# One product of every second pair of samples, shared with its neighbour's, split into seven products of halves

## The chip, the cores and the metric

The kernel runs on 1 core of a Trainium2 chip. The metric is the device time of one execution in microseconds (us). Everything is float32 apart from the zeros that clear PSUM banks.

## The reference, cut to what matters

128 samples of shape 128 x 1024 go through two layers. In each layer a sample uses the weights of its role (1 or 2 of 3 in these inputs):

```python
h = gelu(x @ W_down[role] + b_down[role])      # 128x1024 @ 1024x512
y = x + h @ W_up[role] + b_up[role]            # 128x512 @ 512x1024
out = (y - mean(y)) * rsqrt(var(y) + 1e-5) * gamma[role] + beta[role]
```

The result of layer 0 is the input of layer 1.

## The kernel before

Samples are sorted by role on the chip. Each layer has two stages. The **down stage** makes h for octets of samples (and a few left over) and stores it to DRAM transposed ("hq", "hp"). The **up stage**, which the change touches, takes the samples in 65 items `m` (`NSEQ`, `class Up`): 63 pairs of samples of one role and two single samples (m = 35, 36). Only the first 21 pairs are sure to have the top role; from then on the place of the weights (0, 1 or 2 in `up_blocks`) is read from a table into a register.

The up product of a pair is one level of a Winograd scheme. With A(i,k) half k of sample i's h (128 rows, 256 of the inner dimension) and the weight blocks and their sums B11, B21, T2, T1, T3, B22, T4 (256 x 512 each), a pair makes seven products s1 to s7 instead of eight (`products`, from L937). Each is two TensorE matmuls 128x128 by 128x512 (`product`, L878 to L881). s1, s3, s5 and s7 accumulate in one PSUM bank ("b"), s4 and s6 in another ("e"), s2 = A(0,1)*B21 has bank y (`all_banks[6]`) for itself. After every product VectorE adds what the bank holds then to one half (512 columns) of a sample's row block x in SBUF (`begin` L989, `end` L997; `end` also sums the row for the mean). So the next product into a bank has to wait until VectorE has read it. The sum s2 goes to one place only, the left half of the first sample.

Around the products of a pair stand these steps:

- `load` (L908): h from DRAM, by the queue of SP. `load_rest` (L916): the two samples' x, also by SP.
- `winograd_sums` (L873 to L876): four sums of halves of h on GpSimd (POOL); the second one is made in place and is an operand of s4.
- `seeded` (L932): ScalarE (ACT) copies the bias into a bank before the first product of the pair in it; for m < 4 TensorE clears the bank first (`cleared`, L152).
- `squares` (L1088 to L1094): per sample, ACT makes the mean and the sum of squares, and POOL the power -0.5 of the variance.
- `scaled` (L1101): VectorE makes (y - mean) * gamma.
- `stored`: of the first sample ACT multiplies by the power (L1108) and POOL adds beta (L1109); of the second VectorE does both in one instruction (L1111). `away` (L1116 or L306): SP stores the result.

The order of the instructions on each engine is written out: every step is put on a list with a time (`at(time, step)`), the list is sorted, and each engine runs its steps in that order. One unit of that list is 1/7 of a pair's place: `up_base` grows by 7 per pair, while a pair's products stand at +0, +2, ... +12, so the products of two neighbouring pairs alternate on TensorE.

PSUM has eight banks, s to z. "b" goes round over s, t, u and "e" over v, w, x. Each of the four blocks of SBUF that hold a pair's h has 256 columns at its end that nothing uses.

During the first half of layer 0's up stage the kernel also prepares layer 1's down weights (`DownHalf`: eight groups of four sums on POOL, L361 to L364; loads and stores by SP; copies by ACT and sums by VectorE, L379 and L384), during the second half layer 1's up weights (`UpHalf`: ACT and VectorE).

Of the kernel before, what the change touches and what calls it, by code (L numbers as in the profile page):

```python
# [10 lines left out]
F32 = mybir.dt.float32  # L11
# [9 lines left out]
P = 128  # L21
# [6 lines left out]
def kernel(  # L28
# [38 lines left out]
    NSTAGED = 5  # L67
    staged = region("staged", NSTAGED * 1024)

    hd = {}  # L70
# [5 lines left out]
    for s in range(2):  # L76
# [10 lines left out]
    up_scratch = [  # L87
        {t: dram.tile([R, P, 1024], F32, tag=f"u{layer}{t}", name=f"u{layer}{t}") for t in ORDER}
        for layer in range(2)
    ]  # L90
# [387 lines left out]

    def wu(name, place, j):
        at = ORDER.index(name) * 1024 + j * K  # L480
        if isinstance(place, int):
            return up_blocks[:, place, at : at + K]
        return up_blocks[:, ds(place, 1), at : at + K]

# [106 lines left out]

    plain_blocks = {}

    class PlainItem:
# [18 lines left out]
        def prepare(self):  # L613
            self.bias = new_bias(self.layer, None if self.slots[0] < 2 else self.slots[0], self.tag)
            first = turn_of["results"] % 2
            k = (first, 1 - first, 2)[self.nth % 3]
            self.h = results[:, ts(k, 2048)][:, 0 : 4 * self.n].rearrange("p (f c) -> p f c", f=4)
            self.one = len(self.slots) == 1
            if self.one:
                self.bank = all_banks[(2, 0)[self.parity]]  # L620
                self.ps = [self.bank[:, ts(f, P)] for f in range(4)]
            else:
                self.ps = [all_banks[k] for k in ((6, 7, 1, 3), (2, 0, 4, 5))[self.parity]]

# [246 lines left out]
    def winograd_sums(dst, a, engine=nc.gpsimd):  # L871
# [4 lines left out]
        nc.gpsimd.tensor_tensor(dst[:, 2], a12, dst[:, 0], sub)  # L876

    def product(ps, a, w, place, start=False):  # L878
        for j in range(2):
            nc.tensor.matmul(  # L880
                ps, a[:, j], wu(w, place, j), start=start and j == 0, stop=j == 1, skip_group_check=True  # L881
            )

    before_last = []

    class Up:
        def __init__(self, layer, m):
# [8 lines left out]
            self.before_last = layer == 1 and m == NSEQ - 2  # L896

        def load(self):
            n = self.ns * P
# [9 lines left out]

        def load_rest(self):  # L910
            if self.ns == 1:
                self.x = staged[:, 2048 * (self.slot % 2) :][:, 0:1024].rearrange("p (s n) -> p s n", s=1)
            else:
                self.x = up_block("x", self.pair % 3).rearrange("p (s n) -> p s n", s=2)
            for s, src in enumerate(x_of(self.layer, self.slots, ENG.SP)):
                nc.sync.dma_start(self.x[:, s], src)  # L916

# [9 lines left out]
        def seeded(self, t):  # L927
            spare = self.m == 36 and t == "b"
            ps = all_banks[7] if spare else bank(t)
            if self.m < 4 or spare:  # L930
                cleared(ps)
            nc.scalar.copy(ps, self.t["bias"][:, ts("be".index(t), K)])  # L932
            self.ps[t] = ps

        def products(self):
# [39 lines left out]
            def t4():  # L975
                product(ps["e"], A(0, 1), "B22", self.place)
                self.end(0, 1, ps["e"])

            seeds = [(-3.4 if self.m == 0 else -4, lambda: self.seeded("b")), ({35: -1.65, 36: -0.65}.get(self.m, 1.5), lambda: self.seeded("e"))]
            if self.ns == 2:  # L980
                return list(zip(range(0, 14, 2), (s1, s2, s3, s4, s5, s6, s7))) + seeds
# [17 lines left out]
        def finish_last(self):  # L999
# [29 lines left out]
            def begin_bank(item, s, cols, t):  # L1029
                begun[item.m, cols.start] = ps = bank(t)  # L1030
                nc.scalar.copy(ps, item.t["beta"][:, cols])

# [41 lines left out]
        def finish(self):  # L1074
            if self.last:
                return self.finish_last()
            steps = []
            ending = self.layer == 0 and self.m >= NSEQ - 3
            for s in range(self.ns):
                t = (10.4, 12.4)[s] if self.ns == 2 else 6.4  # L1080
# [24 lines left out]
                def stored(s=s, box=box):  # L1105
                    o, v = box["o"], box["v"][:, 0:1]
                    if s == 0 and not self.before_last and not ending:
                        nc.scalar.mul(o, o, v)  # L1108
# [11 lines left out]

                steps += [(t, squares), (t + 1.3, scaled)]
                if ending:
                    steps += [(t + (2.5, 4.65)[s], stored), (t + (3.6, 5.6)[s], away)]
                    continue
                if not (self.before_last and s == 1):
                    steps.append((t + (3.2 if self.before_last else 3.1), stored))
                    steps.append((t + (5.4, 4.2)[s], away))
            return steps
# [15 lines left out]
    for layer in range(2):  # L1144
# [122 lines left out]
        for m in range(NSEQ):  # L1267
            base = up_base[m]
            item = Up(layer, m)
            at(base - 11.5, item.load)  # L1270
            at(base - 7, item.load_rest)

# [6 lines left out]
            if m >= NSEQ - 4:  # L1279
                at(base + 12.9, lambda p=item.pair: up_done("h", p % 4))  # L1280
                if m >= NSEQ - 3:
                    at(base + 17.2, lambda p=item.pair: up_done("x", p % 3))
# [4 lines left out]
            def known(box=box, m=m):  # L1287
                box["r"] = reg(role_at, SEQ[m], [ENG.SP], R - 1)
                box["c"] = reg(two_changed, m, [ENG.SP], 1)

            prev2 = up_base[m - 2]
            at(prev2 + 2.5, known)
            two_pair = SEQ[m - 2] < SLOT_ONE
            for which, time in (
# [7 lines left out]
                )  # L1302

        if layer == 0:
            for part in range(4):
# [80 lines left out]
```

## Time and profile before

| | |
|---|---|
| median of 3 runs | 2996.15 us (2995.8 to 2997.61) |
| the profiled execution: its time | 2997.57 us |
| the profiled execution: its span (first to last instruction) | 2995.2 us |
| TensorE (PE) busy | 2972.2 us |
| VectorE (DVE) busy | 2316.3 us |
| GpSimd (POOL) busy | 2202.6 us |
| ScalarE (ACT) busy | 1285.1 us |
| granted TensorE clock, mean | 0.998 |
| up stage of layer 0 | about 733 to 1510 us |
| up stage of layer 1 | about 2210 to 2986 us |

A float32 matmul shows as two records (MATMUL) with a weight load each (LDWEIGHTS, on "PEld"). The records of successive matmuls overlap, since their ends are modelled, so the cost of a matmul is read from the starts of successive ones, not from the duration of one. In an answer of the timeline the columns are the start, the length, engine, line and operation, the tiles, and how many were merged.

### The profile page before, as it was taken

The page shows a single profiled execution, that of the slowest core. Times are in us where ns is not written, and L with a number is a line of the kernel's source. Part 1 is how long each engine was busy: PE and PEld are TensorE (multiplying, and loading weights), DVE is VectorE, ACT ScalarE, POOL GpSimd, SP SyncE. Part 2 cuts the span into 40 slices and gives each one's busy share as a digit, 9 for nine tenths or more (in the row PEclk, how much of TensorE's full clock was granted, in tenths as well). Part 3 has the DMA queues.
Part 4 walks back from the last instruction along what each step waited for, and adds up shares of the span by engine and source line. Part 5 has one row for each costly group of instructions (what it writes and reads, how often), then busy time and mean ns, then how long its engine had stood idle before and what let it go on. Part 6 is the DMA issues. An engine that isn't in the chain of part 4 may idle for free. (4 is left out here: it accounts for less than half of the span.)

```text
span 2995.2 us, 43088 instructions
## 1 busy us (share of the span) xinstructions
PE 2972.2 (99%) x10284; PEld 1931.4 (64%) x10294; DVE 2316.3 (77%) x4230; ACT 1285.1 (43%) x2832; POOL 2202.6 (74%) x1965
## 2 busy tenths in 40 slices
PE   8999999999999999999999999999999999999999
PEld 6988888887444444444489888888864444444443
DVE  5498988885787787888855888888857777777777
ACT  1144443333555555555522333333335455554554
POOL 2399998886787887777714888888867777767775
PEclk9999999999999999999999999999999999999999
DMA  8789888445878887988797445675476666777664
GB/s 186 199 234 269 269 258 252 149 148 203 293 257 274 268 289 275 314 294 279 258 257 180 144 146 152 183 206 143 132 265 229 221 220 223 276 247 249 221 220 173
DMA packets 379888, 677.96 MB, mean 226 GB/s; under 512 B 39149, under 2 KB 263662, under 8 KB 379642
## 3 DMA queue, kind: packets, MB, share of 16 engines
q1 hardware_dynamic: 372770, 664.67, 70.0%
q0 software_dynamic: 3072, 8.39, 1.2%
q10 hardware_dynamic: 3800, 2.16, 0.3%
q8 instruction: 88, 1.44, 0.2%
q14 instruction: 158, 1.29, 0.1%
HBM read 676.63 MB, written 249.06 MB: 309 GB/s over the span
## 5 line engine op out<-in xcount | busy, mean ns | idle before, releaser
L1094 POOL TENSOR_TENSOR varu<-varu,mhalf 128x1 f32<-128x1 f32 x254 | 320.5, 1262 | 388.1 <-ACT varu L1093 382.2
L1101 DVE SCALAR_TENSOR_TENSOR units<-blocks,meanu,results 128x1024 f32<-128x1024 f32 x249 | 325.8, 1308 | 169.8 <-ACT units L1092 169.5
L579 DVE STREAM_TRANSPOSE blocks<-staged 128x512 f32<-128x512 f32 x400 | 274.7, 697 | 113.2 <-PE bank_x L630 33.4
L1088 ACT ACTIVATE partu<-statu 128x2 f32<-128x2 f32 x254 | 51.6, 203 | 688.8 <-DVE blocks L997 683.9
L880 PE MATMUL bank_u<-wall,blocks 128*128 (+1 forms) x704 | 330.9, 592 | 0.0
L880 PE MATMUL bank_s<-wall,blocks 128*128 (+1 forms) x672 | 316.0, 592 | 0.7 <-ACT bank_s L932 0.4
L763 ACT ACTIVATE results<-results,bcolo 128x256 f32<-128x256 f32 x448 | 227.4, 508 | 206.6 <-DVE results L781 115.3
L1109 POOL TENSOR_TENSOR units<-units,results 128x1024 f32<-128x1024 f32 x125 | 301.8, 2414 | 3.5 <-ACT units L1108 3.5
L880 PE MATMUL bank_t<-wall,blocks 128*128 (+1 forms) x640 | 301.0, 592 | 0.1
L715 POOL TENSOR_TENSOR units<-blocks 128x512 f32<-128x512 f32 x196 | 250.4, 1278 | 68.0 <-DVE blocks L703 44.8
L1111 DVE SCALAR_TENSOR_TENSOR units<-units,varu,results 128x1024 f32<-128x1024 f32 x128 | 294.6, 2302 | 1.3 <-POOL varu L1094 1.3
L1092 ACT ACTIVATE units<-blocks,meanu 128x1024 f32<-128x1024 f32 x250 | 287.1, 1148 | 8.4
L724 POOL TENSOR_TENSOR units<-blocks,units 128x512 f32<-128x512 f32 x196 | 250.4, 1278 | 14.6 <-PE bank_w L730 3.5
L880 PEld LDWEIGHTS bank_u<-wall,blocks 128*128 128x128 f32 x704 | 133.6, 190 | 166.3 <-issue 156.2
L880 PE MATMUL bank_y<-wall,blocks 128*128 (+1 forms) x504 | 236.8, 592 | 0.2
L880 PEld LDWEIGHTS bank_s<-wall,blocks 128*128 128x128 f32 x672 | 127.4, 190 | 161.7 <-issue 150.7
L880 PEld LDWEIGHTS bank_t<-wall,blocks 128*128 128x128 f32 x640 | 121.3, 190 | 153.7 <-issue 143.8
L873 POOL TENSOR_TENSOR blocks<-blocks 128x256 f32<-128x256 f32 x126 | 193.9, 1539 | 24.2 <-DMA blocks<-hq 21.9
L730 PE MATMUL bank_y<-blocks,wall 128*128 128x256 f32 x784 | 201.2, 379 | 0.0
L880 PEld LDWEIGHTS bank_y<-wall,blocks 128*128 128x128 f32 x504 | 95.8, 190 | 119.1 <-issue 118.7
L880 PE MATMUL bank_x<-wall,blocks 128*128 (+1 forms) x352 | 165.4, 592 | 0.0
L730 PEld LDWEIGHTS bank_y<-blocks,wall 128*128 128x128 f32 x784 | 149.0, 190 | 20.3
(310 smaller groups left out, 6570.3 us busy)
## 6 DMA issues: line engine op xcount, KB each, us to landing
staged<-in_x_dram SPq DMA_DIRECT2D x512, 128.0 KB
mid<-units SPq DMA_DIRECT2D x128, 512.0 KB
staged<-mid SPq DMA_DIRECT2D x512, 128.0 KB
blocks<-in_x_dram SPq DMA_DIRECT2D x126, 512.0 KB
blocks<-mid SPq DMA_DIRECT2D x126, 512.0 KB
out_dram<-units SPq DMA_DIRECT2D x125, 512.0 KB
hq<-results SPq DMA_DIRECT2D x112, 512.0 KB
blocks<-hq SPq DMA_DIRECT2D x112, 512.0 KB
```

What stands on the lines that cost most here:

```text
L579: nc.vector.transpose(to[:, :, at_col : at_col + P].rearrange("p j (a t) -> p j a t", t=SQ), v[:, k])
L715: engine.tensor_tensor(d["d1"], m(0, 0), m(1, 0), sub)
L724: engine.tensor_tensor(d["d2"], m(0, 1), d["d0"], sub)
L730: nc.tensor.matmul(ps[:, 0:256], u, v[:, j], start=start and j == 0, stop=stop and j == 1, skip_group_check=True)
L763: nc.scalar.activation(y, y, AF.Gelu, bias=self.bias[:, f : f + 1])
L873: engine.tensor_tensor(dst[:, 1], a11, a21, sub)
L880: nc.tensor.matmul(ps, a[:, j], wu(w, place, j), start=start and j == 0, stop=j == 1, skip_group_check=True)
L1092: nc.scalar.activation(box["o"], self.x[:, s], AF.Square, bias=m, accum_out=v)
L1094: nc.gpsimd.tensor_tensor(v, v, mhalf[:, 0:1], ALU.pow)
L1101: nc.vector.scalar_tensor_tensor(box["o"], self.x[:, s], box["m"][:, 0:1], self.t["gamma"], add, mul)
L1109: nc.gpsimd.tensor_tensor(o, o, self.t["beta"], add)
L1111: nc.vector.scalar_tensor_tensor(o, o, v, self.t["beta"], mul, add)
```

## The change

25 times per layer two neighbouring pairs, the first with odd m (5, 7, ... 27 and 39, 41, ... 63), share their products s2. Both are a left operand 128x256 with the same right operand B21 of 256 x 512; one above the other they are a product 256x256 by 256x512, and that is made as seven products of halves: left operands 128x128, right operands 128x256 (`class Shared`). The four sums of the left operands are made on POOL in a new region `shared_d`; of the right operands, three are quarters of B21 and four are sums t1 to t4, which lie in the free columns of the four h blocks. The sums are made once per place of the weights: for place 0 on the spot, for places 1 and 2 POOL makes them in passing and SP stores them to DRAM; from m = 21 on the first pair of each couple reloads them, each load under the condition that the role changed. The seven products use the next bank of "e", the next of "b" and bank y. ACT copies the first product from one bank to the other. VectorE adds the banks to the left halves of the first samples of both pairs in six additions 128x256.

With that the order of the pairs' other six products changes: the first pair begins with s4 and makes s1 at +6, after the additions of the shared products, since s1 is now the one that finishes the left half (`s1_end`). The first pair's last steps change places: its first sample is finished by VectorE, its second by ACT and POOL (`by_pool`). The second pair's h is loaded earlier, its x loads are apart, and its `scaled` steps stand later. A bank in which only 256 columns were begun is cleared by TensorE before a pair uses it whole again (`whole`). In layer 1 the banks of the first left-over pairs of the down stage, which ran in fixed banks, are chosen so as to avoid those last used.

```diff
+    class Shared:
+        UNITS = ("t1", "t3", "t2", "t4")
+        d = shared_d.rearrange("p (u c) -> p u c", c=P)
...
+        @classmethod
+        def reload(cls, layer, place, cond):
+            for u in range(4):
+                src = shared_scratch[layer][u][ds(place, 1)].rearrange("o p n -> p (o n)")
+                nc.sync.dma_start(cls.tail(u), src, cond=cond, cond_hint=False)
...
+        def m(self, i, k):
+            return (self.first, self.second)[i].a[:, 0, 2 + k]
+        def begin(self):
+            b, e = bank("e"), bank("b")
+            begun_in_part.extend((b, e))
+            self.ps = {"b": b[:, 0:UNIT], "x": all_banks[6][:, 0:UNIT], "e": e[:, 0:UNIT]}
+            if self.first.m in (min(SHARED), LATER):
+                cleared(all_banks[6])
+        def inner(self, name):
+            m, d = self.m, self.d
+            k, i0, i1, op = {
+                "d1": (1, lambda: m(0, 0), lambda: m(1, 0), sub),
+                "d3": (3, lambda: m(1, 0), lambda: m(1, 1), add),
+                "d0": (0, lambda: d[:, 3], lambda: m(0, 0), sub),
+                "d2": (2, lambda: m(0, 1), lambda: d[:, 0], sub),
+            }[name]
+            nc.gpsimd.tensor_tensor(d[:, k], i0(), i1(), op)
+        def product(self, p):
...
+                "p1": ("b", lambda: m(0, 0), lambda: b(0, 0)),
+                "p2": ("x", lambda: m(0, 1), lambda: b(1, 0)),
+                "p3": ("b", lambda: d[:, 0], lambda: t("t2")),
+                "p4": ("e", lambda: d[:, 3], lambda: t("t1")),
+                "p5": ("b", lambda: d[:, 1], lambda: t("t3")),
+                "p6": ("e", lambda: d[:, 2], lambda: b(1, 1)),
+                "p7": ("b", lambda: m(1, 1), lambda: t("t4")),
+            }[p]
+            nc.tensor.matmul(self.ps[to], v(), w(), start=p in ("p1", "p4"), stop=True, skip_group_check=True)
+        def carry(self):
+            nc.scalar.copy(self.ps["x"], self.ps["b"])
+        def flow(self, t, i, h):
+            y = (self.first, self.second)[i].x[:, 0, ts(h, UNIT)]
+            tt(y, self.ps[t], y, add)
+        def steps(self):
+            s = [(-1.9, self.begin), (2.3, self.carry)]
+            s += [(-2.4 + 0.1 * k, lambda n=n: self.inner(n)) for k, n in enumerate(("d3", "d0", "d1", "d2"))]
+            for p, t in dict(p1=2, p4=3.1, p3=4, p2=4.1, p5=5.3, p6=5.4, p7=6.5).items():
+                s.append((t, lambda p=p: self.product(p)))
+            for t, args in (
+                (3.2, ("e", 1, 1)), (4.3, ("b", 0, 1)), (4.4, ("x", 0, 0)),
+                (5.5, ("b", 1, 1)), (5.6, ("e", 0, 1)), (6.6, ("b", 1, 0)),
+            ):
+                s.append((t, lambda args=args: self.flow(*args)))
+            return s
+    LATER = 39
+    SHARED = list(range(5, 29, 2)) + list(range(LATER, NSEQ, 2))
...
         def seeded(self, t):
             ps = all_banks[7] if spare else bank(t)
+            whole(ps)
...
+            def s1_end():
+                product(ps["b"], A(0, 0), "B11", self.place)
+                self.end(0, 0, ps["b"])
+            if self.coupled(0):
+                seeds = [(2, lambda: self.seeded("b")), (-2, lambda: self.seeded("e"))]
+                return [(0, s4), (6, s1_end), (8, s3), (9.5, s6), (10, s5), (12, s7)] + seeds
...
+            if self.coupled(1):
+                seeds[0] = (-1.7, seeds[0][1])
+                return list(zip((0, 2, 4, 8, 10, 12), (s1_end, s3, s4, s5, s6, s7))) + seeds
...
+            by_pool = 1 if self.coupled(0) else 0
...
-                    if s == 0 and not self.before_last and not ending:
+                    if s == by_pool and not self.before_last and not ending:
                         nc.scalar.mul(o, o, v)
                         nc.gpsimd.tensor_tensor(o, o, self.t["beta"], add)
...
-                steps += [(t, squares), (t + 1.3, scaled)]
+                late = self.coupled(1) and self.m + 1 in SHARED
+                steps += [(t, squares), (t + ((2.3, 1.5)[s] if late else 1.3), scaled)]
...
-                    steps.append((t + (3.2 if self.before_last else 3.1), stored))
-                    steps.append((t + (5.4, 4.2)[s], away))
+                    wait = 3.2 if self.before_last else 3.95 if s and by_pool else 3.1
+                    steps.append((t + wait, stored))
+                    steps.append((t + ((6.2 if s else 5.4) if s == by_pool else 4.2), away))
...
-            at(base - 11.5, item.load)
-            at(base - 7, item.load_rest)
+            at(base - (13 if item.coupled(1) else 11.5), item.load)
+            if item.coupled(1):
+                at(base - 9, lambda item=item: item.load_rest((0,)))
+                at(base - 7, lambda item=item: item.load_rest((1,)))
+                for time, step in Shared(before, item).steps():
+                    at(base - 7 + time, step)
+            else:
+                at(base - 7, item.load_rest)
```

## The prediction

> **What bounds the kernel now.** I read the page's busy times first, then TensorE's waits, then the timelines of TensorE, VectorE and POOL in the up stage.
>
> ```profile
> PE 2972.2 (99%) x10284; PEld 1931.4 (64%) x10294; DVE 2316.3 (77%) x4230; ACT 1285.1 (43%) x2832; POOL 2202.6 (74%) x1965
> ```
>
> TensorE is busy all the time. Its waits in all of layer 0's up stage (729 to 1510 us) are these three, in us, times, longest:
>
> ```profile
> PE bank_t L630 <- DVE blocks L997: 1.1, 1, 1.1
> PE bank_s L880 <- ACT bank_s L932: 0.4, 1, 0.4
> PE bank_s L880 <- DVE blocks L989: 0.2, 1, 0.2
> ```
>
> So work taken from TensorE there is time gained, as long as no other engine makes it wait. The second resource shows in the timelines of VectorE and POOL, here in layer 1:
>
> ```profile
> 2414.48 1.28 DVE L1101 SCALAR_TENSOR_TENSOR units<-blocks,meanu,results 128x1024 f32<-128x1024 f32 x1 [0.49 <-ACT units L1092]
> ...
> 2417.34 2.23 DVE L1111 SCALAR_TENSOR_TENSOR units<-units,varu,results 128x1024 f32<-128x1024 f32 x1
> 2419.50 0.68 DVE L997 SCALAR_TENSOR_TENSOR blocks<-bank_y,blocks 128x512 f32<-128x512 f32 x1
> ```
>
> ```profile
> 2414.86 1.32 POOL L1094 TENSOR_TENSOR varu<-varu,mhalf 128x1 f32<-128x1 f32 x1 [2.44 <-ACT varu L1093]
> 2416.15 2.35 POOL L1109 TENSOR_TENSOR units<-units,results 128x1024 f32<-128x1024 f32 x1
> 2418.46 1.71 POOL L873 TENSOR_TENSOR blocks<-blocks 128x256 f32<-128x256 f32 x1
> 2420.24 0.73 POOL L874 TENSOR_TENSOR blocks<-blocks 128x256 f32<-128x256 f32 x1
> ```
>
> L1111 takes 1.24 us at its shortest (over all its records), here 2.23: it starts at 2417.34, while POOL's L1109 runs to 2418.50, and only then gets through. POOL's L873, behind it, takes 1.71 instead of 0.73, the difference being what was left of L1111. L1094 is 1.32 beside L1101 and 0.54 at its shortest. So VectorE's L1101 and L1111, which read two tensors in SBUF, and POOL's instructions exclude each other; I call this **the lock**. The additions from PSUM (L997, L989) stay at 0.68 whatever POOL does.
>
> **TensorE's part.** Two matmuls 128x512 (one product) and two 128x256:
>
> ```profile
> 900.52 1.88 PE L880 MATMUL bank_y<-wall,blocks 128*128 128x512 f32 x4
> 902.24 1.88 PE L880 MATMUL bank_x<-wall,blocks 128*128 128x512 f32 x4
> ```
>
> ```profile
> 561.34 1.03 PE L730 MATMUL bank_s<-units,wall 128*128 128x256 f32 x4
> 562.21 1.03 PE L730 MATMUL bank_w<-units,wall 128*128 128x256 f32 x4
> ```
>
> Start to start 1.717 us (over ten such steps), so 0.8585 per matmul of 512 columns; 0.863 for two of 256, so 0.4316 each. A couple loses four of the first kind, 3.434 us, and gets seven of the second, 3.021: **0.413 us less**. 25 couples in each layer, 50 in all: 20.6 us less. TensorE's order in the changed kernel has 350 matmuls in the new class, seven times 50, and 58 clears instead of 46. A clear takes 0.21 us (743.23 to the next start at 743.44): 12 x 0.21 = 2.5 us more. Net **-18.1 us**, if TensorE never waits more than now.
>
> The Trainium skill ("TensorE: Matmul & The Clock Gate", section "The mechanism") says that a weight load overlaps matmuls in flight only when the row group differs. That speaks against more, shorter matmuls on the full array: 14 records per couple instead of 8, each with a load of 190 ns, would cost 6 x 0.19 = 1.14 us more, and the change would lose (1.14 - 0.413) x 50 = 36 us. The rows deny it here: matmul records of 256 columns follow every 0.216 us with a load of 0.190 each, all hidden.
>
> **Does TensorE wait?** I lay a couple out with t = 0 at the start of the first pair's s4. F and G are its pairs, F' and G' those of the couple before. TensorE's order is: F s4 0, G' s5 1.72, p1 3.43, G' s6 3.87, p4 5.58, p3 6.01, p2 6.45, G' s7 6.88, p5 8.59, p6 9.03, F s1 9.46, p7 11.17, G s1 11.61, F s3 13.32, G s3 15.04, F s6 16.76, F s5 18.47, G s4 20.19, F s7 21.91, next couple 23.62 (24.03 now). A product can be read 0.21 us after its last start plus step (the modelled end 1.88 - 1.717, and 0.05 to VectorE's start). VectorE moves on 0.61 us after an addition of 512 columns and about 0.34 after one of 256 (L781, same kind and shape, lasts 0.41), 1.2 after L1101 or L1111. From the sum of a row to the scaled step 1.87 us pass, to POOL's power 2.25 (2412.61 to 2414.48 and 2414.86).
>
> - VectorE loses two additions of 512 and gains six of 256 per couple: 6 x 0.34 - 2 x 0.61 = 0.8 us on 19.3 busy in 24.03. Hidden if the order is right: F' stored 1.65 to 2.8 (behind POOL's sums), F' second scaled 3.3 to 4.5, F s4 to 5.1, G' s5 to 5.7, which G' s7 needs at 6.88; shared additions 6.4 to 7.4; G' s7 to 9.4; two shared to 10.1; scaled G' behind L1109 10.45 to 11.65; F s1 to 12.26, needed at 13.32; p7's, then the second scaled G', behind a power, 12.8 to 14.0; G s1 to 14.68, which **G s3 needs at 15.04: 0.36 us to spare**, the least of all. Elsewhere it is 0.65 to 1.4.
> - The copy p1 to bank y on ACT (L757, same shape, 0.36 us) fits between 4.1 and 4.5; p3 needs it at 6.01. The seed of G's bank s has to come between VectorE's G' s7 (9.49) and G s1 (11.61): 0.57 us, ready at 10.1. But in ACT's queue it stands behind the multiplication for F' (waiting for POOL's power, ready at 5.0) and G' squares; a POOL 2 us late delays it.
> - POOL gains four sums 128x128 per couple. No row shows one; 128x512, 384 and 256 take 1.27, 1.00 and 0.73 us, so between 0.27 (the step alone) and 0.73, and I take the line's 0.46: 1.9 us per couple. They run between -1.5 and 1.7, p4 needs the first at 5.58. With powers at 0.54 the lock is held 8 x 0.73 + 4 x 0.54 + 2 x 2.35 + 1.9 by POOL and 6 x 1.2 by VectorE = 21.8 of 23.62 us. By the layout POOL still idles 1.7 to 3.7, 12.8 to 13.3 and 20.6 to 21.6, some 3 us, and the sums of h that the next s4 needs are made 4 us early.
> - SP: G's h is loaded 1.5 units (2.6 us) earlier, behind four conditional reloads in the 17 couples from m = 21 (0.08 us when skipped, 0.34 when run, by L502's rows). G's first x waits for F's scaled step (done at 0.7) and is needed at 6.4, where now x has some 12 us. A load of 512 KB landed 7 us after its issue at 848.69, in a stretch with all DMA engines busy; alone, at the 400 GB/s that such stretches reach, its bytes take 1.3. In layer 1, with the DMA share at 0.66, I cost this at nothing.
>
> So a plain couple costs no wait. **The first run of layer 0** (m = 5 to 28) has more: 24 sums of `DownHalf` (twelve of 1.27, twelve of 1.00) and ten sums of weights (0.73), 34.5 us in 12 couples, against 12 x 3 = 36 us of idle POOL. Now POOL is busy 0.83 of the time there and TensorE doesn't wait. About six couples hold four `DownHalf` sums each, some 4.6 us against 3 idle: POOL is 1.6 to 6 us late there, L1109 collides with the scaled steps before F s3 and G s3, and SP's stores of these sums (waits of up to 4.8 us for L364 now) hold up x behind them. Between 0 (all caught in the idle) and 18 us (only half of the idle is usable) I take 1 us for each of the six, 6 us, nearer the lower end since the needed sums are 4 us early. For layer 1's ten sums of weights and `UpHalf`'s VectorE sums (0.68 each, some falling on the 0.36) 1 us together. The waits at L630 (1.1) may go, or be replaced.
>
> **The sum:** 2997.57 - 20.6 + 2.5 + 6 + 1 = 2986.5 for the profiled execution, which lay 1.42 above the median. Against the median of 2996.15: **2985**.
>
> **The rivals.**
> 1. *No waits at all*: POOL's lateness is absorbed. 2996.15 - 18.1 = 2978. For it: the spare 4 us on everything that TensorE takes from POOL. Chance 0.27.
> 2. *The lock is full.* Half of POOL's idle in layer 0's first run can't be used, or the 0.36 us at G s3 is 0.36 too small in every couple: 18 us of waits, 2996. For it: 21.8 of 23.62 us held, gaps of 0.08 between POOL's instructions not counted. Against: neither queue is short of work while the other holds the lock. Chance 0.18, over 2990 to 3002.
> 3. *Slower*: L1109 of G' takes the lock just ahead of VectorE's second scaled step. VectorE gets there at 12.6, ACT frees L1109 at 13.3; from 0.7 us of delay on, the step waits 2.3 us more, G s1 is read at 17.5 and G s3 waits 2.5. In the 12 couples of layer 0's first run that is 30 us: 2996.15 - 18.1 + 30 = 3008. Chance 0.13.
>
> The forecast itself (3 to 12 us of waits, 2981 to 2990) has 0.42. That the sharing doesn't happen is ruled out by the 350 matmuls.
>
> **The range** reaches from 2977 (no waits, and L630's gone) to 2999, which leaves out rival 3 and the top of rival 2. About 0.2% (6 us) is what a measurement of this kernel can tell from no change. Faster by more: forecast and rival 1, 0.69; within: rival 2, 0.18; slower: 0.13.
>
> **What would show it.** Right: in layer 1 new matmuls 0.43 us apart, a couple in 23.6 us, no waits of PE at L981; in layer 0 waits of 0.3 to 3 us between m = 5 and 28, on ACT's seed, VectorE's additions or POOL. POOL busy 2202 + 50 x 1.9 + 28 x 0.73 = about 2320 us. Wrong: waits in every couple (G s3, s <- DVE), or waits for DMA at the shared additions of the second pair.

## The result, and the profile after

The changed kernel took **3043.19 us** (median of 4 runs, 3037.19 to 3045.86) against 2995.98 for the kernel before, measured beside it: ratio 1.0154, 95% interval 1.0142 to 1.0166. It is 47.2 us slower where the prediction had 11 us faster, and outside the range. The profiled execution took 3043.54 us, its span is 3041.9.

The page's busy times of the changed kernel (in the line after the span):

```profile
PE 2976.1 (98%) x10593; PEld 1992.6 (66%) x10606; DVE 2306.4 (76%) x4430; ACT 1306.7 (43%) x2882; POOL 2242.8 (74%) x2193
```

TensorE has fewer columns to do and is not less busy. The two stages tell more. TensorE's waits in layer 0's up stage were three rows with 1.7 us in sum. They are now nine rows with 37.9 us, of which the first six are (us, times, longest):

```profile
PE bank_w L981 <- DVE blocks L988: 12.8, 6, 5.7
PE bank_s L899 <- DVE blocks L1133: 7.2, 10, 1.4
PE bank_w L981 <- issue: 5.1, 1, 5.1
PE bank_x L981 <- issue: 4.7, 3, 3.8
PE bank_x L981 <- POOL blocks L885: 3.0, 1, 3.0
PE bank_x L981 <- POOL units L1247: 2.9, 1, 2.9
```

Of the 37.9 us, 29.2 stand in front of L981, the shared products. In the same stage VectorE has a row that did not exist before (L988 is the shared addition), and SP has three that are new or grew (before: L447, now L452, 12.3; L502, now L507, behind POOL 5.5; no L937):

```profile
DVE blocks L988 <- DMA blocks<-in_x_dram: 39.9, 13, 6.5
```

```profile
SPq L507 <- POOL units L1247: 36.0, 15, 6.4
SPq L937 <- POOL shared_d L923: 24.1, 8, 9.2
SPq L452 <- POOL staged L369: 20.5, 6, 6.1
```

So VectorE waits for G's x, and the queue of SP, which fetches x and h, itself stands for POOL. SP stood for POOL before, too: its stores of the results waited 99.8 us there (L1116) and wait 58.2 now (L1254). The sum of these rows went from 117.6 to 138.8 us only; what is new is which loads stand behind such a wait. In layer 1 the steady state is as foretold. The first lines of the timeline of TensorE from 2863.8 and from 2887.4 on:

```profile
2863.48 0.59 PE L899 MATMUL bank_s<-wall,blocks 128*128 x1
2863.91 0.59 PE L981 MATMUL bank_x<-wall,blocks 128*128 x2
2864.34 1.88 PE L899 MATMUL bank_v<-wall,blocks 128*128 x4
```

```profile
2887.53 0.59 PE L981 MATMUL bank_x<-wall,blocks 128*128 x2
2887.96 1.88 PE L899 MATMUL bank_v<-wall,blocks 128*128 x4
```

From p1 to the next p1 is 23.62 us, and p1 lasts 0.43. This gives an account that carries the rest of the text: for every couple but the last of a run the time from its p1 to the next one's, less 23.62 (the "excess"). In the changed kernel these are, in us:

```
layer 0, m = 5 to 27:   1.69 9.04 2.41 0.00 2.95 6.30 0.71 0.00 1.46 2.05 8.64            sum 35.3
layer 0, m = 39 to 63:  4.58 0.37 6.45 0.03 0.48 0.00 5.94 0.00 0.42 0.00 0.91 0.26       sum 19.4
layer 1, m = 5 to 27:   0.44 1.75 1.24 0.00 0.77 0.76 0.00 0.00 0.00 0.00 0.00            sum  5.0
layer 1, m = 39 to 63:  5.67 and eleven times 0.00                                        sum  5.7
```

Together 65.4; and -18.1 (the prediction's TensorE part) + 65.4 = +47.3. The medians differ by 47.2 and the two profiled spans by 46.7 (2995.2 to 3041.9), so the account closes within 1 us.

Only 43.6 of the 65.4 are waits that the profile lists (37.9 in layer 0, 5.7 in layer 1). The rest follows them. TensorE's timeline in layer 1's first couple of the second run:

```profile
2718.99 0.70 PE L981 MATMUL bank_t<-blocks,shared_d 128*128 128x256 f32 x2 [0.17 <-POOL shared_d L966]
...
2725.57 0.67 PE L981 MATMUL bank_x<-blocks,shared_d 128*128 128x256 f32 x2 [3.20 <-POOL blocks L884]
2726.08 0.59 PE L981 MATMUL bank_t<-wall,shared_d 128*128 x2
2726.51 3.55 PE L899 MATMUL bank_u<-wall,blocks 128*128 x4
2729.85 0.66 PE L981 MATMUL bank_x<-blocks 128*128 128x256 f32 x2
```

The row of the 3.20 us names L884, which had ended at 2724.77; what ended last in front of it was VectorE's addition from bank x (L988, 2725.06 to 2725.47). After the wait the product of bank u takes 3.34 us from start to start instead of 1.72. The granted clock says why; the windows' columns are busy times, then clock, DMA share and GB/s:

```profile
2685.00:2710.00 25.00, 25.00 (x60) 11.12 (x59) 16.50 (x27) 12.58 (x26) 17.74 (x15) 1.00 0.61 206
2710.00:2735.00 25.00, 21.64 (x54) 10.13 (x53) 17.27 (x28) 11.26 (x25) 15.20 (x15) 0.93 0.74 253
2735.00:2760.00 25.00, 25.00 (x67) 12.37 (x66) 19.18 (x34) 12.66 (x27) 19.93 (x21) 1.00 0.88 297
```

From 2726.6 to 2729.9 alone the clock is 0.50. 0.07 of 25 us is 1.7 us. In layer 0 six such stretches lie between 740 and 1535. Taken in windows of 8 us around them the clock is 0.57 once and 0.79 five times (before: 1.00 throughout), so they cost at most 0.43 x 8 + 5 x 0.21 x 8 = 12 us, less where TensorE stood still in them. At least 8 of the 22 us that are not listed as waits are left without an account. The Trainium skill ("TensorE: Matmul & The Clock Gate", section "What's actually happening") gives half speed after an idle window of about 3.4 us and full speed after as long a busy one. This trace agrees with the halving. It does not agree with the length of the idle time: waits of 3.20 us here and of 2.93 us in layer 0 were enough.

### The profile page after: what moved, and what is told of

Its sections match the earlier page's. It is cut to its first block, busy times and chain, and to the rows that moved or that the text cites. A ratio compares the mean times of both kernels' runs of the same rounds, so it can differ in the third digit from the quotient of the medians.

```text
span 3041.9 us, 44667 instructions
## 1 busy us (share of the span) xinstructions
PE 2976.1 (98%) x10593; PEld 1992.6 (66%) x10606; DVE 2306.4 (76%) x4430; ACT 1306.7 (43%) x2882; POOL 2242.8 (74%) x2193
## 5 line engine op out<-in xcount | busy, mean ns | idle before, releaser
L1232 POOL TENSOR_TENSOR varu<-varu,mhalf 128x1 f32<-128x1 f32 x254 | 246.5, 971 | 298.1 <-ACT varu L1231 293.0
L899 PE MATMUL bank_s<-wall,blocks 128*128 (+1 forms) x960 | 452.4, 593 | 8.4 <-DVE blocks L1133 8.1
L899 PE MATMUL bank_u<-wall,blocks 128*128 (+1 forms) x960 | 459.2, 601 | 0.7 <-DVE blocks L1133 0.7
L1247 POOL TENSOR_TENSOR units<-units,results 128x1024 f32<-128x1024 f32 x125 | 310.2, 2482 | 26.3 <-ACT units L1246 26.3
L899 PEld LDWEIGHTS bank_u<-wall,blocks 128*128 128x128 f32 x960 | 184.7, 193 | 212.7 <-issue 200.8
L899 PEld LDWEIGHTS bank_s<-wall,blocks 128*128 128x128 f32 x960 | 180.9, 190 | 199.1 <-issue 179.3
L1249 DVE SCALAR_TENSOR_TENSOR units<-units,varu,results 128x1024 f32<-128x1024 f32 x128 | 221.0, 1726 | 11.4 <-POOL varu L1232 11.3
L899 PE MATMUL bank_v<-wall,blocks 128*128 (+1 forms) x464 | 218.2, 592 | 0.8 <-POOL blocks L885 0.8
L1246 ACT ACTIVATE units<-units,varu 128x1024 f32<-128x1024 f32 x125 | 142.7, 1142 | 63.6 <-POOL varu L1232 62.0
L1133 DVE SCALAR_TENSOR_TENSOR blocks<-bank_u,blocks 128x512 f32<-128x512 f32 x170 | 116.6, 686 | 60.2 <-PE bank_u L899 59.1
L899 PEld LDWEIGHTS bank_v<-wall,blocks 128*128 128x128 f32 x464 | 88.0, 190 | 100.3 <-issue 83.9
L732 POOL TENSOR_TENSOR units<-units,blocks 128x512 f32<-128x512 f32 x84 | 107.1, 1276 | 60.8 <-PE bank_s L741 20.5
```

What stands on the lines that cost most here:

```text
L899: nc.tensor.matmul(ps, a[:, j], wu(w, place, j), start=start and j == 0, stop=j == 1, skip_group_check=True)
L1232: nc.gpsimd.tensor_tensor(v, v, mhalf[:, 0:1], ALU.pow)
L1247: nc.gpsimd.tensor_tensor(o, o, self.t["beta"], add)
L1249: nc.vector.scalar_tensor_tensor(o, o, v, self.t["beta"], mul, add)
```

## What came too late, in the trace

Before the experiments, three places where the chain can be read. **Layer 1, a new store in front of a load** (nothing is prepared there). SP, and then POOL:

```profile
2332.99 1.03 SPq L937 DMA_DIRECT2D s<-shared_d  x2
2334.59 0.10 SPq L493 DMA_DIRECT2D wall<-u1T  x1
2334.78 0.80 SPq L1041 DMA_DIRECT2D blocks<-mid  x2
2335.68 0.52 SPq L1033 DMA_DIRECT2D blocks<-hq  x1
```

```profile
2331.26 2.40 POOL L923 TENSOR_TENSOR shared_d<-wall 128x256 f32<-128x256 f32 x2
...
2342.96 0.46 POOL L966 TENSOR_TENSOR shared_d<-blocks 128x128 f32<-128x128 f32 x1 [5.68 <-DMA blocks<-hq]
```

SP's L937 stores the new sums of weights and cannot be issued before POOL has made them (L923); SP had issued nothing since 2322.39. Behind it stands L1033, G's h, of which POOL makes the sums d (L966): they wait 5.68 us. p4, p3, p5 and p6 need d.

**The second run's first couple.** G's h is issued behind the couple's four reloads (L943) at 2712.37, and POOL shows

```profile
2718.48 0.46 POOL L966 TENSOR_TENSOR shared_d<-blocks 128x128 f32<-128x128 f32 x1 [6.30 <-DMA blocks<-hq]
...
2720.26 0.55 POOL L1232 TENSOR_TENSOR varu<-varu,mhalf 128x1 f32<-128x1 f32 x1
```

Behind the late sums in POOL's queue stands the power of the next sample; VectorE's L1249 waits for it (3.43 us) and then lasts 3.35 us beside POOL's L1247. VectorE's shared additions stand behind it, and TensorE behind these (the 3.20 above).

**Layer 0, m = 7.** SP's waits between 795 and 829 us are led by three for POOL:

```profile
SPq L452 <- POOL staged L369: 4.8, 1, 4.8
SPq L1254 <- POOL units L1247: 4.7, 1, 4.7
SPq L937 <- POOL shared_d L923: 3.6, 2, 3.4
```

They end at 812.9. What stood behind them follows in a bunch, F's two x at 815.2, then nine stores from 816.6 to 825.3, and G's first x only behind these; and POOL has itself stopped for one of the nine (d1B):

```profile
824.91 0.39 SPq L452 DMA_DIRECT2D d1B<-staged  x1
826.50 0.37 SPq L1041 DMA_DIRECT2D blocks<-in_x_dram  x1
```

```profile
827.55 0.99 POOL L366 TENSOR_TENSOR staged<-staged 128x384 f32<-128x384 f32 x1 [5.39 <-DMA d1B<-staged]
```

```profile
831.28 0.42 DVE L988 TENSOR_TENSOR blocks<-bank_t,blocks 128x256 f32<-128x256 f32 x1 [6.19 <-DMA blocks<-in_x_dram]
```

```profile
832.18 1.19 PE L981 MATMUL bank_w<-blocks,shared_d 128*128 128x256 f32 x2 [5.66 <-DVE blocks L988]
...
834.01 2.67 PE L899 MATMUL bank_u<-wall,blocks 128*128 128x512 f32 x4
```

SP waits for POOL, POOL waits for SP's store, and x, behind both in SP's queue, comes late.

## The experiments

Theory A: G's first x comes late in layer 0, and no more. Theory B: the lock (VectorE and POOL exclude each other, as in the prediction) leaves POOL no idle time. Theory C, formed after the first four runs: the in-order queue of SP hands over *both* early loads of a couple, G's h (for d) and G's first x, late, because stores that wait for POOL stand ahead of them. Kernels of one group ran beside the same runs of the kernel before. The sums are those of the couples' excesses in the profiled execution; layer 1's column takes both of its runs of couples together. after_no_prep, before_no_prep, no_down_prep and no_prep_with_loads leave out work that layer 1 needs, so they show times only.

| run | us, ratio to before, 95% | layer 0, m 5 to 27 | layer 0, m 39 to 63 | layer 1 |
|---|---|---|---|---|
| changed kernel | 3043.19, 1.0154 (1.0142 to 1.0166) | 35.3 | 19.4 | 10.7 |
| x0_by_act | 3039.2, 1.0146 (1.013 to 1.0163) | 27.5 | 20.4 | 12.3 |
| fourth_x_block | 3035.29, 1.0123 (1.0106 to 1.014) | 31.5 | 20.1 | 8.4 |
| after_no_prep | 2999.55, 1.0006 (0.9997 to 1.0016) | 7.2 | 6.9 | 10.8 |
| before_no_prep | 2993.51, 0.9991 (0.9981 to 1.0001) | | | |
| layer1_only | 3000.28, 1.001 (1.0001 to 1.002) | | | 13.9 |
| h_before_stores | 3025.43, 1.0095 (1.008 to 1.0111) | 32.7 | 14.7 | 0.9 |
| h_and_x0 | 3012.46, 1.0058 (1.0042 to 1.0073) | 22.4 | 11.6 | 0.9 |
| layer1_h_before_stores | **2988.12, 0.9972 (0.9962 to 0.9983)** | | | 0.9 |
| stores_by_pool | 3065.25, 1.0233 (1.0216 to 1.025) | 50.4 | 18.1 | 8.2 |
| h_x0_and_stores_by_pool | 3051.55, 1.0179 (1.0162 to 1.0196) | 49.1 | 16.0 | 2.9 |
| layer1_first_by_pool | 3011.99, 1.0055 (1.0039 to 1.0072) | | | 21.7 |
| down_gap | 3003.47, 1.002 (1.0009 to 1.0031) | 15.1 | 15.3 | 0.9 |
| down_sums_by_vector | 3016.26, 1.0061 (1.0044 to 1.0077) | 27.4 | 13.6 | 0.9 |
| no_down_prep | 2989.9, 0.9977 (0.9967 to 0.9986) | 0.5 | 11.9 | 0.9 |
| no_prep_with_loads | 2978.49, 0.9939 (0.9922 to 0.9955) | 0.7 | 0.4 | 0.9 |

### First group: x alone, and no preparation

**x0_by_act.** G's first x by ScalarE's queue:

```diff
-                at(base - 9, lambda item=item: item.load_rest((0,)))
+                at(base - 8.65, lambda item=item: item.load_rest((0,), nc.scalar, ENG.Activation))
```

> The change, with one edit: the x of the first sample of each second pair is loaded by ScalarE's queue, at a place in ScalarE's order where it idles, instead of SP's; the transfer, its size and the block it needs stay. Theory A (x comes late: in the changed kernel VectorE waits 39.9 us in layer 0 for this load, 13 times, and TensorE some 25 us behind it, because SP issues it late behind other steps): the waits for this x in layer 0 fall from 39.9 to under 12 us, TensorE's idle time there by some 20 us, time 3010 to 3025 us. Theory B (my prediction's: POOL is late and holds the lock, the wait for x is only where it shows): the waits move to other instructions, time 3038 to 3046 us.

3039.2 us, where theory B had it. VectorE's waits for x shrank from 42 us to 9, and TensorE's went to other rows (L981 behind L966: 8.3 us; L899 behind L1133: 8.4), while POOL's waits for hq before L966 grew from 35.7 to 56.5 us. Theory A falls in its narrow form: with x in time, the sums d wait for h.

**fourth_x_block.** A fourth block for x in the place of the third place's weights:

```diff
-                self.x = up_block("x", self.pair % 3).rearrange(...)
+                self.x = (fourth_x if self.pair % 4 == 3 else up_block("x", self.pair % 4)).rearrange(...)
```

> The change, with a fourth block of SBUF for x (in the place of the third role's up weights, which no sample of these inputs has; their loads and sums are left out, which none of the outputs needs). So no load of x waits for the step 'scaled' of three items before. Theory A: the waits of VectorE for x are all but gone, 3043 falls by the 25 us of TensorE's waits behind them and by some 8 us of slow clock after them: 3000 to 3015 us. Theory B: the lock and POOL's lateness are untouched, 3035 us or more.

3035.29 us, at the lower end of theory B's "3035 us or more"; VectorE still waits 34.2 us for x (8 times, up to 8.1). A free block does not help when the load stands in a queue. The third place's sums fall away in this kernel, too. What of the 8 us that it gained comes from that, and what from the block, no run parts.

**after_no_prep** and **before_no_prep.** No `DownHalf(1)` and `UpHalf(1)` in layer 0's up stage.

> The changed kernel without the preparation of layer 1's weights in layer 0's up stage (left out; layer 1 then runs with layer 0's sums). To be compared with the kernel before with the same left out. Theory A, with SP's queue and the transfers of the preparation as what makes x late: layer 0 behaves as layer 1 does, where the change cost 2.3 us net, so the two differ by 0 to +8 us. If the ring of three x blocks alone makes x late: +25 us or more. Theory B: POOL has no sums to be late with, -5 to -18 us.

> The kernel before without the preparation of layer 1's weights (left out; layer 1 runs with layer 0's sums). TensorE waits for nothing in the up stages before, so nothing to gain there: 2992 to 2997 us by every theory.

2999.55 and 2993.51: without the preparation the change costs 6.0 us instead of 47.2. So 41 us are its collision with the preparation, and 24.9 us of excess against 18.1 of gain are there without it, 14.1 in layer 0 and 10.8 in layer 1. Theory B, which had this pair at -5 to -18 us, falls as the whole cause: the loss of 6 us is there without POOL's preparing sums, and in the changed kernel 17 of the 23 steps from couple to couple in layer 1 have an excess of 0.00. How much of the 41 us is POOL's own load these two do not say; the fourth group goes on from there.

### Second group: which load, which layer

> The change in layer 1's up stage alone; layer 0 keeps 7 products of each pair. Theory C (in layer 0 SP hands over G's h and G's first x late, behind stores of the preparation): layer 0 loses nothing, layer 1 keeps the +2.3 us that its last stage showed in the trace after, so 2996 to 3000. Theory B (the lock between VectorE and POOL costs each dense couple): also +2. A gain of 9 us (2987) would say that layer 1's waits come from layer 0's lateness.

**layer1_only** (`COUPLED = (1,)`): 3000.28 us, 0.3 above the range. Layer 0 loses nothing, layer 1 keeps its own 13.9 - 9.1 = +4.8 (measured: +3.8).

**h_before_stores:** one number.

```diff
-            at(base - (13 if item.coupled(1) else 11.5), item.load)
+            at(base - (14.4 if item.coupled(1) else 11.5), item.load)
```

> Both layers; G's h load is put 1.4 units earlier on SP, ahead of the stores of the new weight sums (which wait for POOL's subtractions) and ahead of the four reloads at the start of the second run. In layer 1 of the trace after, couples 1 to 6 took 5 us and the first couple of the second run 5.7 us more than 23.62, and before each of those waits POOL's sums d waited for hq (5.7 and 3.7 us). Theory C: these 10.6 us of layer 1 go but for some 2, the like 12 to 14 us of layer 0 go too, and some of the 40 of the preparation: 3010 to 3025. Theory B (POOL late by its own work and the lock, its new subtractions first): unchanged, 3037 to 3045.

3025.43 us, 18 us less, 0.4 above the expected range. Layer 1's excess falls from 10.7 to 0.9: nearly all of its loss was G's h behind what stood ahead of it on SP, the stores of the sums or, at the second run, the reloads. In the couple shown above, POOL's first rows of d no longer name hq:

```profile
2327.95 1.44 POOL L966 TENSOR_TENSOR shared_d<-blocks 128x128 f32<-128x128 f32 x1
2329.46 0.46 POOL L966 TENSOR_TENSOR shared_d<-shared_d,blocks 128x128 f32<-128x128 f32 x1
```

Counted from the weights' sums (2321.97 here, 2331.26 there) d starts 5.98 us later instead of 11.70. The load itself is issued 8.54 us before those sums (2313.43) instead of 4.42 after them (2335.68). That is 13 us for a step of 1.4 units, which are 2.4 us on the list: what counted was the place in the queue. Layer 0 gains 7 us only; its x is as late as before (VectorE behind x: 36.0 us).

**layer1_h_before_stores:** both edits.

> The change in layer 1 alone with G's h load 1.4 units earlier. Theory C: layer 1 gets its 25 couples at 23.62 us with 2 us of waits or less, so the 9.1 us of its matmuls less clears, less 2: 2987 to 2990, faster than before. Theory B: as layer1_only, 2996 to 3000.

**2988.12 us, faster than both kernels.** TensorE's waits in all of layer 1's up stage are one, at the end of the kernel:

```profile
PE bank_t L1172 <- POOL units L1237: 0.9, 1, 0.9
```

**h_and_x0:** h_before_stores and x0_by_act together.

> As h_before_stores, and G's first x goes by ScalarE's queue. Theory C says that each load alone left the other late; with both out of the way of SP's stores layer 0 keeps only POOL's own lateness: 2995 to 3010. If it stays above 3025, the stores of the preparation reach TensorE by another way (tables, POOL's late seconds).

3012.46 us, a miss by 2.5 above the range, but 13 us under h_before_stores, where the same move of x without that of h had given 4. Each load helps little while the other is late. The Trainium skill ("DMA: Bandwidth & Descriptors", section "Issuing engines are not separate DMA queues") says that issuing from several engines saves only the issuing time, which is usually small. Here the other queue saved 13 us, and the traces show them as waits in SP's order (VectorE behind x: 36.0 us before this edit). No run here tests what that section says of the DMA engines that all queues share.

### Third group: the stores, and the change's second half

**stores_by_pool** and **h_x0_and_stores_by_pool:** `DownHalf(1)`'s stores and those of the weights' sums on GpSimd's own queue, without and with the two loads (the lines show the stores of the weights' sums; those of `DownHalf` are changed likewise).

```diff
-                    nc.sync.dma_start(shared_scratch[layer][cls.UNITS.index(name)][place], at[name])
+                    nc.gpsimd.dma_start(shared_scratch[layer][cls.UNITS.index(name)][place], at[name])
```

> The change as it is, except that the stores of the down weights prepared for layer 1 (in layer 0's up stage) and of the new sums of the weights for places 1 and 2 go by GpSimd's own queue, so that SP no longer waits for GpSimd there (L452 20.5 us and L937 24.1 us of SP's waits in the trace after); loads stay where they were. Theory C: couples 1 to 6 of layer 1 lose their 4.9 us again, the second run's first couple keeps its 5.7 (its reloads are still ahead of G's h), and layer 0 keeps what UpHalf's stores, tables and late x make: 3010 to 3028. If SP's waits for GpSimd are not what makes the loads late: 3037 to 3048, and GpSimd's issuing makes it worse.

> h_and_x0 and these stores by GpSimd's queue. In h_and_x0 the longest delay left (9.3 us in layer 0's second couple) came from GpSimd standing 6.1 us before one of its preparing sums for a store that SP had issued late, and being 6 us late for 20 us more. Theory C: this goes, and layer 0 keeps 10 to 20 us of the 35 left: 2990 to 3003. If GpSimd's lateness is its own load: 3008 to 3018.

3065.25 and 3051.55 us: both misses, 22 and 39 us slower than the same kernels with these stores on SP. The rows of the changed line in stores_by_pool (shortest, median, longest in ns) tell why:

```profile
L450 POOL DMA_DIRECT2D d1T<-staged x16: 725/741/757, 808.6 to 1176.0; - x16
...
L450 POOL DMA_DIRECT2D d1B<-staged x12: 715/742/762, 821.7 to 1142.1; - x12
```

Each store takes 0.74 us of POOL itself (the queue of SP showed 0.4 to 1.0, of SP's time). The 56 of `DownHalf` and 8 of the weights' sums (0.57 us each) are some 46 us of POOL in layer 0's first run, and POOL had none to spare there: POOL's lateness goes on to VectorE (L1250 behind POOL's power: 53.2 us in the second kernel). So these two could not tell what they were made for. In layer 1, where only the eight stores of the weights' sums are moved, m = 5 to 27 fell from 5.0 to 2.4 us.

**layer1_first_by_pool:** layer1_h_before_stores without the change of places in the last steps.

```diff
-            by_pool = 1 if self.coupled(0) else 0
+            by_pool = 0
```

> As layer1_h_before_stores (2988.1), without the change's second half: in couples, too, the first sample's last steps stay with ScalarE and GpSimd and the second sample's with VectorE, as in the kernel before. Theory C says nothing of it. By the prediction's part on the last steps, the first sample's 2.3 us addition on GpSimd then stands in front of the sums d, and VectorE's 1.2 us run of the second sample beside GpSimd's work: from nothing up to 13 couples at 1 us, 2988 to 3001.

3011.99 us, 23.9 more, above the expected range: 1.0 us in nearly every couple, each time TensorE behind POOL's four sums of h, which now stand behind the first sample's L1247:

```profile
PE bank_x L981 <- POOL blocks L884: 6.2, 8, 0.8
PE bank_w L981 <- POOL blocks L885: 4.9, 7, 0.8
PE bank_x L981 <- POOL blocks L885: 3.1, 4, 0.8
PE bank_w L981 <- POOL blocks L884: 3.1, 4, 0.8
```

(Waits of 0.8 us at the longest; their sum is 17.3 of the 22.7 us that layer 1's couples and the pairs between them took over.) That is a wait for the sums of h, where the expectation had the sums d. Without the change of places this kernel is 16 us slower than the kernel before, although G's h is early in it.

### Fourth group: what layer 0 still loses

All four start from h_and_x0, whose longest excess (9.3 us) began with this row of POOL, the only wait for such a store in layer 0's up stage there:

```profile
826.16 0.99 POOL L366 TENSOR_TENSOR staged<-staged 128x384 f32<-128x384 f32 x1 [6.07 <-DMA d1B<-staged]
```

**down_gap:** the second group of `DownHalf(1)`'s sums 6 units later.

```diff
-                for time, step in job.over_bank(start + 10, 2) + job.rest(start + 24, 2.5, 1.2, 8):
+                for time, step in job.over_bank(start + 10, 2) + job.rest(start + 24, 2.5, 1.2, 14):
```

> As h_and_x0 (3012.5), with the second group of GpSimd's preparing sums 6 units (10 us) later behind the first, so that they do not stand for the first group's stores. If those stalls (6.1 us at the longest, 4 in all) make GpSimd late: 3000 to 3007. If GpSimd is late by its load as such: within 4 us of 3012.

3003.47 us, as expected if the stall for that store is what makes POOL late, and POOL has no wait for such a store left in that stage. The edit also moves the sums themselves by 10 us, and no run parts the two. (Its runs spread from 3000.93 to 3011.16 and the profiled one is the longest, so its sums in the table are some 8 us above its median.)

**down_sums_by_vector:** `nc.gpsimd` to `nc.vector` for these sums in layer 1's weights.

> As h_and_x0, with the 32 preparing sums of the down weights for layer 1 (128x384, 1.0 us each on GpSimd) on VectorE. If GpSimd's lateness in the first run of layer 0 is what is left there (20 us of the 35 in couples 1 to 12): 2993 to 3003. If VectorE is as tight as GpSimd there, so that the sums only change their place: 3008 to 3025.

3016.26 us: the load only changes its place (half of these sums are 128x512, 1.27 us each, and not 128x384); VectorE, behind the same stores, holds TensorE instead (L899 behind L1133: 14.8 us, up to 4.3).

**no_down_prep** and **no_prep_with_loads.**

> As h_and_x0, but the preparation of layer 1's down weights is left out in layer 0's up stage (layer 1 uses layer 0's down sums); that of its up weights stays. Of the 35 us by which layer 0's couples were over 23.62 us in h_and_x0, couples 1 to 12 had 22 and the second run 13. If the first run's part is the down preparation: 2988 to 2994.

> As h_and_x0, and both preparations are left out of layer 0's up stage (layer 1 uses layer 0's sums). The kernel before without them ran 2993.5; the change without waits takes 18.1 us off that, and with some 2 us of waits left: 2975 to 2979. Above 2985 the two loads would not be all that the change lacks without preparation.

2989.9 and 2978.49 us, both as expected. Without the down preparation the first run keeps 0.5 of its 22.4 us; without the other, too, the second run keeps 0.4. TensorE's waits in layer 0's up stage are then two:

```profile
PE bank_u L899 <- DVE blocks L1133: 0.3, 1, 0.3
PE bank_s L899 <- DVE blocks L1133: 0.2, 1, 0.2
```

2978.49 is 15.0 under before_no_prep; -18.1 + 2.0 of excess makes -16.1.

With the table these give a two by two of the total excess: 65.4 us as it is, 34.9 with the two loads moved (h_and_x0), 24.9 without the preparation, 2.0 with both. So moving the loads takes off 30.5 us beside the preparation and 22.9 without it, and even with both loads in time the preparation costs 32.9 us.

In layer 0's second run h_and_x0 keeps 11.6 us beside `UpHalf`. No run parts `UpHalf`'s loads, stores, copies and sums, but the trace shows the chain of the largest excess there (7.2 us):

```profile
1355.99 0.40 SPq L471 DMA_DIRECT2D staged<-in_L_cond_W_up_dram  x1
1361.61 0.59 ACT L384 COPY bank_z<-staged 128x512 f32<-128x512 f32 x1 [4.39 <-DMA staged<-in_L_cond_W_up_dram]
1362.23 0.69 DVE L389 TENSOR_TENSOR staged<-bank_z,staged 128x512 f32<-128x512 f32 x1 [4.64 <-ACT bank_z L384]
1363.31 1.22 PE L981 MATMUL bank_x<-blocks 128*128 128x256 f32 x2 [3.87 <-DVE blocks L988]
```

`UpHalf`'s load of raw weights (L471) is one more load that comes late: it is issued behind the four reloads (L943, 1346.50 to 1352.86) and lands 5.6 us later. ACT's copy and VectorE's sum (L389) stand for it, and the shared additions L988 stand behind that sum in VectorE's order. What stays open is the rest of that run, and how much of the first run's 22.4 us is POOL's own load.

## Why the prediction was wrong

- **TensorE's part was right.** 0.43 us per pair of short matmuls, 23.62 us per couple, 350 matmuls; no_prep_with_loads is 15.0 us under before_no_prep, where 18.1 less its 2.0 of excess would be 16.1.
- **VectorE's part and the 0.36 us at G s3 were right.** In layer1_h_before_stores no couple waits for VectorE. The sums d took the 0.46 us that was chosen, and 1.44 us when they met VectorE.
- **The step that failed is SP's:** "G's h is loaded 1.5 units (2.6 us) earlier, behind four conditional reloads", and of both loads, in layer 1, "I cost this at nothing." It priced what the reloads take (0.08 to 0.34 us each) and the transfer (1.3 to 7 us), and not the instruction ahead in SP's queue that *waits*: L937, which the change itself adds and which stands for POOL's L923. In layer 1 the excess was 10.7 us, and moving this load alone brings that down to 0.9. The "needed at 6.4" was the due time of x; h had no due time in the prediction at all.
- **Layer 0's terms were mis-sized, in part by the same step.** "I take 1 us for each of the six, 6 us, nearer the lower end since the needed sums are 4 us early" is for the first run, which measured 35.3. The second run, with `UpHalf`, stood in the "1 us together" with layer 1 and measured 19.4. The sums d were not early, since their operand came late; SP's stores were named as holding up x, but only as a consequence of POOL's lateness, inside the same 6 us. The traces show SP and POOL holding each other: a sum stands for a store, the store's queue for POOL. Of the 54.7 us the loads moved alone leave 34.0, the preparation left out alone leaves 14.1, both together 1.1. So late h and x are some 21 us of it, and the preparation costs more than 30 even when they are in time. Of that, down_gap took 9 (with it POOL's stall for a store), and one late load of `UpHalf` cost 7.2; what POOL's own load costs is not shown.
- **A wait was priced at its length.** About 22 of 65.4 us are not listed as waits; the stretches of half clock account for at most 12 in layer 0 and 1.7 in layer 1.
- **The rivals.** "The lock is full" (2996) falls in the form that costs every couple: with the loads in time and nothing prepared, layer 0's 25 couples run with 1.1 us of excess in all, lock and all. Its other form, idle time of POOL that `DownHalf`'s sums cannot use, and the slower rival (3008, L1109 ahead of the scaled step) are not ruled out by that run, which has no such sums; they could be part of the 22.4 us that h_and_x0 keeps in the first run. That slower was possible was seen, the main mechanism not. The sign named for being wrong, "waits for DMA at the shared additions of the second pair", is the one that came.
- **POOL's busy time** was 2242.8, not 2320. VectorE and POOL meet less often, which the prediction did not count: VectorE's L1111 lasted 2.30 us in the mean and L1249 lasts 1.73, the power 1.26 and now 0.97, the first sum of h 1.54 and now 0.99. The change of places does a good part of this: in layer 1 alone, layer1_first_by_pool has 2.30, 1.23 and 1.51, and layer1_h_before_stores, with it, 2.05, 1.13 and 1.18.

## What to carry to other kernels

When a change makes a load earlier or its data needed earlier, walk the issuing queue backwards from that load to the first instruction that waits for another engine, and give that wait a price, beside that of the transfer (in the couple of layer 1 shown above SP stood for 10.6 us, and the load landed 7.3 us after its issue). A store of something that a busy engine makes should stand behind the loads that the same engine's next work needs. Here a wait of TensorE cost about one and a half times its listed length (65.4 us of excess for 43.6 of waits).

## What the runs showed of the hardware

- A DMA issued by GpSimd occupied GpSimd for 0.74 us for such strided stores (128 x 2 x 256 float32, stores_by_pool), which made a queue "of its own" the dearest place for them.
- In the changed kernel's up stages the granted clock fell to 0.50 for 3.4 us, once for 6.8, during or just behind each of the seven waits of TensorE of 2.93 to 5.66 us, and behind none of those up to 1.97 us. In it products took up to twice their time (1.72 us became 3.34, two short matmuls 0.43 became 0.98). The edge is not sharp over all runs: in h_and_x0 a wait of 2.50 us had it and one of 2.21 had not, and in after_no_prep one of 3.20 us had not.
